# Spectral convolution: one column transform per group, and the first scale moved inside a group

## The chip, the cores and the metric

The kernel runs on one core of a Trainium2 chip. A core has five engines that work side by side, each from its own queue: TensorE (PE, with its weight loads PEld), VectorE (DVE), ScalarE (ACT), GpSimd (POOL) and SyncE (SP), which here only issues DMAs. The metric is the device time of one execution in microseconds (us). Times quoted from the profile are of one profiled execution, counted from the start of its span.

## The reference

Four layers in a row, each `x + layer(groupnorm(x))`, on x of 8 images, 32 channels, 256 × 256, float32:

1. a Fourier layer: two-dimensional real FFT, the lowest 32 × 32 frequencies of two corners mixed over the channels by complex weights, inverse FFT, plus a bias;
2. a 5 × 5 convolution with one kernel for all channels, padding 2;
3. a gated recurrence (GRU) along the image's width;
4. running maxima from four sides, mixed with x by a 1 × 1 convolution.

The group norm has 16 groups of two channels and takes mean and variance over a group's two channels and all pixels:

```python
def _gn(v, G=16, eps=1e-5):
    g = v.reshape(B_, G, C_ // G, H_, W_)
    m = jnp.mean(g, axis=(2, 3, 4), keepdims=True)
    s = jnp.var(g, axis=(2, 3, 4), keepdims=True)
    return ((g - m) / jnp.sqrt(s + eps)).reshape(v.shape)
x = x + _L0_conv_ref(_gn(x), ...)
x = x + _L1_conv_ref(_gn(x), L1_conv_kernel, 1, 2)
```

What the change touches is the end of layer 1 (the inverse transform) and the whole of layer 2 (the 5 × 5 convolution), which the kernel does in one stage.

## The kernel before

Stages follow each other: `forward_and_mix` (forward FFT and mixing, written to the scratch tensor smd), `inverse_and_conv` (the one concerned, about 305 to 1156 us of the span, its repeated part from 365 us), `recurrence` (to about 2530 us) and `maxima_and_mix`.

`inverse_and_conv` works on 16 *units*. A unit is half of one image's channels, 16 of them, in two channel halves `ch` of 8. A channel half lies in one of five large buffers (`x1s`, used in turn), laid out as nine *blocks* of 32 columns of the image on the partitions (four row phases `a` times 32), with 28 columns of progress from block to block, so that each block carries the margin that a 5 × 5 kernel needs.

For each unit:

- `load_spectrum` (once per image, so every second unit) brings the mixed spectrum from smd through SP's queue; `spectrum` then works on it with a few small VectorE instructions and one matmul, y0 (L367).
- `over_rows` (four calls of two channels) is the inverse transform along rows: four matmuls into tp (L407), copied to tt by ACT (L414).
- `over_columns` (one call per block p, called by `transform`) is the inverse transform along columns: eight matmuls into two PSUM banks "up" (L424), one per channel half, and then two VectorE additions (L433) that add the input x (loaded as xb through POOL's queue, L386) and write block p of the two x1 buffers. For p = 0 `transform` also issues eight small squares on ACT (L450), and for p = 2, 5 and 8 it starts the loads of a piece of x for the unit after (L386).
- `squares` sums x1² over blocks on ACT (L450), four activations (one per channel pair) per call. `scale` sums these over the partitions by matmuls into v (L457), adds eps on VectorE (ve, L461) and raises to the power −0.5 on POOL (r, L463). `r` is what the convolution's result is multiplied by; `spectrum` has already taken the mean out of the zero frequency.
- `conv(u, ch, g)` is one *group*: the 5 × 5 convolution of the two channels of pair g, as 18 tile matmuls of 64 × 64 on both halves of the array (L490, 36 instructions) into three banks vp, in an order of tiles written by hand and with a semaphore of its own. Five VectorE instructions (L527), called the *update* below, multiply by r, add to x1 in place and sum. A unit has eight groups: g = 0 to 3 for ch 0, 4 to 7 for ch 1.
- `squares2` (three ACT instructions, L534) sums the squares of the result of each group, `statistics` and `keep` make the next layer's mean and scale of them (L559 to L578), and `store` writes a channel half to x2d in HBM with 36 DMAs (nine blocks, four row phases a; L547), on SP's queue.

The work of three units overlaps: while unit u is convolved, the columns of unit u+1 are transformed and the rows of unit u+2. The whole stage stands in a `manual_schedule`: each engine executes its instructions in the order in which the program issues them. That order is the loop at the end of the function, over units u and groups g. `PLACES` says after which groups which column transforms of unit u+1 are placed: in the kernel before, one right behind the group's tiles, and in groups 1 to 3 a second one later in the same group. Unit u+1's first scale comes after group 7 of unit u, its second in group 1 of unit u+1 itself.

PSUM's eight banks are given by tags: four for vp, two for up, one for tp (tag "s"), one for all small sums (tag "st": v, y0 and the statistics' s). A tile of a tag waits until the reader of the buffer's last tile is done. A transform needs two banks of "up" at once. Likewise, writing a block of x1 waits for the stores that read the same block of the same buffer, five channel halves earlier.

## Time and profile before

| | us |
|---|---|
| median of 3 timed executions (lowest, highest) | 3231.57 (3227.11, 3237.39) |
| the profiled execution: span from first to last instruction | 3226.3 |
| forward transform and mixing, start of the stage | 0 to 365 |
| convolution stage, repeated part with its last stores | 365 to 1156 |
| recurrence | 1160 to 2530 |
| maxima and mixing | 2530 to 3226 |

The profiled execution's own time is given only as its span; the timed executions lie 0.8 to 11.1 us above it. Busy time in the window from 365 to 1160 us (795 us):

| engine | busy us | what fills it |
|---|---|---|
| PE | 727.8 | vp (L490) 453.3; up (L424) 185.7; tp (L407) 60.7 |
| DVE | 549.2 | update (L527) 350.8; sums of transforms (L433) 173.8 |
| ACT | 454.5 | squares2 (L534) 203.6; squares (L450) 166.4 |
| POOL | 113.9 | issue of loads, powers |

How to read the profile: a row of the order of time gives start, length, engine, line, operation, result <- operands, form, the number of merged instructions, and in square brackets how long the engine had stood idle and what released it. PE's busy time overlaps with itself a little, since matmuls are pipelined and their ends are modelled. A window's row gives, after its length, each engine's busy time, then the mean granted clock of TensorE (1.00 is full), the DMA engines' busy share and GB/s. "SPq" rows are DMA issues on SP's queue, from the first issue to the last.

### The profile page before, as it was taken

The numbers are of one execution on the slowest core, as the hardware profiler recorded it, in microseconds if no ns is written. First come the engines' busy times: TensorE is split into PE (matmuls) and PEld (weight loads), VectorE is DVE, ScalarE is ACT, GpSimd is POOL, SyncE is SP. The second block draws the span as 40 slices with busy tenths as digits, with TensorE's granted clock in tenths as the row PEclk, the third lists the DMA queues.
The fourth block names the chain that finished last, engine by engine and source line by source line (L and its number), as shares of the span: only waits on it lengthen the run. The fifth ranks groups of instructions, "written<-read, shape, count | busy, mean of one in ns | idle before, by whom it ended". The sixth has DMA issues, their size and how long they took to land.

```text
span 3226.3 us, 112014 instructions
## 1 busy us (share of the span) xinstructions
PE 2866.3 (89%) x47802; PEld 1666.4 (52%) x47802; DVE 2614.3 (81%) x5188; ACT 1862.5 (58%) x4362; POOL 860.8 (27%) x1241
## 2 busy tenths in 40 slices
PE   7975799999999969999999999999999577777776
PEld 4655344444444446666666666666666233333332
DVE  5742577777767759999999999999999799999998
ACT  3422365565565657888888888888887222222222
POOL 0110011111111145555555555555555200000000
PEclk9985899999999989999999999999999788888998
DMA  9978577888777545665555555666554588878885
GB/s 385 387 288 193 129 187 193 196 194 195 186 182 197 138 110 153 159 159 151 146 148 147 147 146 151 157 159 159 155 143 121 188 306 305 308 311 314 313 308 217
DMA packets 527058, 655.75 MB, mean 203 GB/s; under 512 B 388825, under 2 KB 389737, under 8 KB 500829
## 3 DMA queue, kind: packets, MB, share of 16 engines
q1 hardware_dynamic: 483628, 494.33, 53.9%
q0 software_dynamic: 17200, 85.05, 8.1%
q10 hardware_dynamic: 25728, 69.21, 5.4%
q8 instruction: 374, 6.13, 0.8%
q14 instruction: 128, 1.04, 0.1%
HBM read 371.63 MB, written 272.63 MB: 200 GB/s over the span
## 4 chain that ended last, share of the span: by engine, by line
PE 54%; DVE 25%; DMA 8%; SPq 6%; issue 5%; ACT 2%; POOL 0%; DVEq 0%; ACTq 0%; POOLq 0%
PE r L742 13%; PE z L742 12%; PE ni L742 6%; PE nh L742 6%; DMA x2d<-x 6%; SPq L547 5%; DVE rv L993 5%; PE vp L490 4%; DVE x L527 3%; PE yp L131 3%; DVE dq L1005 2%; DVE m L1009 2%; DVE m L1007 2%; DVE x L1002 2%; DVE m L1008 2%
## 5 line engine op out<-in xcount | busy, mean ns | idle before, releaser
L750 PE MATMUL z<-hs,weights 64*64 64x256 f32 x4080 | 539.4, 382 | 0.0
L750 PE MATMUL r<-hs,weights 64*64 64x256 f32 x4080 | 525.2, 375 | 0.0
L750 PE MATMUL ni<-hs,weights 64*64 64x256 f32 x4080 | 524.9, 375 | 0.0
L832 POOL TENSOR_TENSOR xw<-xw,hs 128x256 f32<-128x256 f32 x496 | 339.5, 684 | 635.6 <-DVE hs L831 635.6
L527 DVE SCALAR_TENSOR_TENSOR x<-vp,r,x 64x512 f32<-64x512 f32 (+2 forms) x640 | 350.8, 563 | 164.6 <-PE vp L490 137.8
L1039 ACT ACTIVATE ot<-o,bres 128x512 f32<-128x512 f32 x256 | 155.4, 690 | 541.5 <-PE o L1023 533.9
L490 PE MATMUL vp<-x,c_conv 64*64 64x384 f32 (+2 forms) x4608 | 457.5, 514 | 0.2
L826 POOL TENSOR_TENSOR a<-zm,xn 128x256 f32<-128x256 f32 x510 | 372.7, 731 | 6.4 <-issue 6.2
L1023 PE MATMUL o<-m,wsc 32*32 32x512 f32 x3072 | 237.1, 830 | 152.9 <-DVE m L1009 106.3
L824 ACT ACTIVATE n<-n,bih 128x256 f32<-128x256 f32 x510 | 260.8, 511 | 184.4 <-DVE n L823 184.4
L490 PEld LDWEIGHTS vp<-x,c_conv 64*64 64x64 f32 x4608 | 238.3, 138 | 234.5 <-issue 128.5
L742 PE MATMUL z<-xn,weights 64*64 64x256 f32 x2040 | 305.3, 376 | 24.2 <-ACT xn L722 24.2
L742 PE MATMUL r<-hs,weights 64*64 64x256 f32 x2040 | 319.0, 389 | 4.4 <-DVE hs L831 3.4
L742 PE MATMUL r<-xn,weights 64*64 64x256 f32 x2040 | 305.6, 376 | 1.0 <-ACT rs L817 1.0
L742 PE MATMUL nh<-xn,weights 64*64 64x256 f32 x2040 | 305.7, 376 | 0.0
L742 PE MATMUL z<-hs,weights 64*64 64x256 f32 x2040 | 305.2, 376 | 0.0
L742 PE MATMUL ni<-hs,weights 64*64 64x256 f32 x2040 | 305.2, 375 | 0.0
L722 ACT ACTIVATE xn<-xw,shift,turned 128x256 f32<-128x256 f32 x496 | 291.9, 589 | 0.0
L750 PEld LDWEIGHTS ni<-hs,weights 64*64 64x64 f32 x4080 | 284.4, 133 | 0.3
L818 DVE SCALAR_TENSOR_TENSOR n<-nh,bhh,rs 128x256 f32<-128x256 f32 x510 | 246.3, 483 | 45.3 <-ACT rs L817 30.7
L750 PEld LDWEIGHTS r<-hs,weights 64*64 64x64 f32 x4080 | 281.1, 131 | 0.2
L817 ACT ACTIVATE rs<-r,brz 128x256 f32<-128x256 f32 x510 | 242.7, 476 | 50.8 <-PE r L750 30.3
(165 smaller groups left out, 6267.2 us busy)
## 6 DMA issues: line engine op xcount, KB each, us to landing
xb<-in_xl_dram POOLq DMA_DIRECT2D x96, 768.0 KB, 6.4
xa<-in_xt_dram SPq DMA_DIRECT2D x64, 1024.0 KB
x<-x3d SPq DMA_DIRECT2D x32, 2048.0 KB
fw<-fwd SPq DMA_DIRECT2D x32, 2048.0 KB
out_dram<-ot ACTq DMA_DIRECT2D x64, 1024.0 KB
xw<-x2d SPq DMA_DIRECT2D x31, 2048.0 KB
fwd<-fm SPq DMA_DIRECT2D x248, 256.0 KB
x3d<-xw SPq DMA_DIRECT2D x248, 256.0 KB
```

Of the source, the lines that this page charges most:

```text
L490: ins = nc.tensor.matmul(vps[bank][to], lhsT=k.conv[r, P : P + 64] if kind == 2 else k.conv[r, o], rhs=pair_of(u, ch, g, lo, hi, (2, 0)[i] ...
L527: nc.vector.scalar_tensor_tensor(x, src[o], r1[rows, g : g + 1], x, ALU.mult, ALU.add, accum_out=s1[rows, 0, n, ch, g : g + 1])
L547: (nc.gpsimd if 2 * u + ch == 2 * n - 1 and p % 2 else nc.sync).dma_start(out=x2d[b, a, c0 : c0 + CH, TS * t + lo : TS * t + hi].rearrange ...
L722: nc.scalar.activation(norms[bi][:, b, w], raws[bi][:, b, w], AF.Identity, bias=shift[:, b : b + 1], scale=sc[:, 1, b : b + 1])
L742: ins = nc.tensor.matmul(out[r], lhsT=weights[r, kind, gate, :], rhs=src[r], start=start, stop=stop)
L750: ins = nc.tensor.matmul(out[pairs[1 - i]], lhsT=weights[r, kind, gate, :], rhs=prev[r, :, q0 : q0 + Q], start=False, stop=stop,)
L817: rs = nc.scalar.activation(r, p["r"], AF.Sigmoid, bias=brz[:, 0:1])
L818: nc.vector.scalar_tensor_tensor(m, p["nh"], bhh[:, 2:3], r, ALU.add, ALU.mult)
L824: nc.scalar.activation(m, m, AF.Tanh, bias=bih[:, 2:3])
L826: product = nc.gpsimd.tensor_tensor(a, zm, cur, ALU.mult)
L832: nc.gpsimd.tensor_tensor(raw, raw, new, ALU.add)
L1023: nc.tensor.matmul(pts[b2][i][32 * j : 32 * j + 32].rearrange("p (w q) -> p w q", q=Q), lhsT=wsc[q, b2, t, :], rhs=src[j][q, b2], start=first,
```

## The change

The order of work in the convolution stage is rearranged:

- `PLACES` becomes one block per group: after group 0 to 6 come blocks 1, 2, 3, 5, 6, 7, 8 of unit u+1. Block 4 is transformed *inside* group 3, between the group's tiles (`between`). Block 0 is begun a group early: of unit u+2, after group 7 of unit u.
- The banks: tp joins the small sums in one bank "st", and "up" gets three instead of two.
- Unit u's scale of channel half 0 is computed inside its own group 0, after 14 of the 18 tiles, and no longer after group 7 of the unit before. It now sums three pieces, so the squares of channel half 0 come in three: block 0, blocks 1 to 5 (in group 4) and blocks 6 to 8 (in group 7), where there were two (block 0, blocks 1 to 8 in group 5).
- `spectrum` moves from group 2 of an even unit to group 7 of the odd one before it (for the first image it stays in group 2 of unit 0), and `load_spectrum` from group 7 of the odd unit to its group 2, so ahead of the store of that unit's first half in SP's queue. `keep` moves by one group.
- A store issues its DMAs block by block, the four row phases of a block after each other; before, it went through all nine blocks for each row phase.

```diff
--- before.py
+++ after.py
@@ -314,7 +314,7 @@
     BANKS = ((0, 2), (2, 6), (6, 9))
     PIECES = ((0, 3), (3, 6), (6, 9))
 
-    PLACES = ((0,), (1, 2), (3, 4), (5, 6), (7,), (8,), (), ())
+    PLACES = (1, 2, 3, 5, 6, 7, 8)
     with ExitStack() as ctx:
         one = ctx.enter_context(tc.tile_pool(name="a2c", bufs=1))
         xp = ctx.enter_context(tc.tile_pool(name="a2x", bufs=1))
@@ -397,7 +397,7 @@
                 r=[None, None],
             )
 
-        def over_rows(u, c, tag="s", bufs=1):
+        def over_rows(u, c, tag="st", bufs=1):
 
 
             b, h = units[u]
@@ -413,7 +413,7 @@
                     )
             nc.scalar.copy(state[u]["tt"][:, :, c : c + 2, :], tp.rearrange("p c (a q) -> p a c q", a=A))
 
-        def over_columns(u, p, tag="up", bufs=2):
+        def over_columns(u, p, tag="up", bufs=3):
 
 
             tt = state[u]["tt"]
@@ -472,7 +472,7 @@
             if some[0]:
                 tc.declare_no_dep(ins.ins, group="conv", reason="later matmuls of the same bank end last")
 
-        def conv(u, ch, g):
+        def conv(u, ch, g, between=()):
 
 
 
@@ -511,6 +511,8 @@
             tiles(0, 1, start=True)
             tiles(2, 0, stop=True, wait=second)
             third = tiles(0, 2, signal=True)
+            for work in between:
+                work()
             tiles(1, 0, stop=True, wait=first)
             tiles(0, 0, stop=True, wait=third)
             s1 = state[u]["s1"]
@@ -541,9 +543,9 @@
         def store(u, ch):
             b, h = units[u]
             c0 = 2 * CH * h + CH * ch
-            for a in range(A):
-                for p, t in enumerate(BLOCKS):
-                    lo, hi = 0 if t == 0 else 2, 32 if t == NT - 1 else 30
+            for p, t in enumerate(BLOCKS):
+                lo, hi = 0 if t == 0 else 2, 32 if t == NT - 1 else 30
+                for a in range(A):
                     (nc.gpsimd if 2 * u + ch == 2 * n - 1 and p % 2 else nc.sync).dma_start(
                         out=x2d[b, a, c0 : c0 + CH, TS * t + lo : TS * t + hi].rearrange("c w q -> w c q"),
                         in_=x1_of(u, ch)[32 * a + lo : 32 * a + hi, p, :, 1 : 1 + Q],
@@ -579,7 +581,7 @@
                     by_pair(stb[:, kind, b, 2 * CH * h : 2 * CH * (h + 1)]), twice(st[:, kind], 2)
                 )
 
-        def transform(u, p, again):
+        def transform(u, p):
             if u:
                 over_columns(u, p)
             else:
@@ -587,10 +589,10 @@
             if p == 0:
                 for ch in range(2):
                     squares(u, ch, 0, 0, 1)
-            if again < n:
+            if u + 1 < n:
                 for i, (_, hi) in enumerate(PIECES):
                     if p == hi - 1:
-                        load(again, i)
+                        load(u + 1, i)
 
         n = len(units)
         with tc.manual_schedule(engines=None):
@@ -602,9 +604,9 @@
             for u in range(2):
                 begin(u)
             for c in range(0, CH, 2):
-                over_rows(0, c, *(("s", 1), ("up", 2))[c // 2 % 2])
+                over_rows(0, c, *(("st", 1), ("up", 3))[c // 2 % 2])
             for p in range(NT):
-                transform(0, p, 1)
+                transform(0, p)
                 if p % 2:
                     over_rows(1, p - 1)
                 if p == 4:
@@ -612,40 +614,49 @@
                         squares(0, ch, 1, 1, 5)
             for ch in range(2):
                 squares(0, ch, 2, 5, NT, ch == 1)
-                scale(0, ch, 3)
+            scale(0, 1, 3)
+            transform(1, 0)
             for u in range(n):
+                more, beyond = u + 1 < n, u + 2 < n
                 for g in range(2 * G):
-                    conv(u, g // G, g % G)
-                    places = PLACES[g] if u + 1 < n else ()
-                    for p in places[:1]:
-                        transform(u + 1, p, u + 2)
-
+                    between = []
+                    if g == 0:
+                        between.append(lambda: scale(u, 0, 3))
+                    if g == 3 and more:
+                        between.append(lambda: transform(u + 1, 4))
+                    conv(u, g // G, g % G, between)
+                    if g < len(PLACES) and more:
+                        transform(u + 1, PLACES[g])
+                    if g == 2 * G - 1 and beyond:
+                        transform(u + 2, 0)
                     if g == 1 and u > 0:
                         scale(u, 1)
-                    if g == 2 and u > 0:
-                        st = statistics(u - 1)
-                    if g == G - 1 and u + 2 < n:
-                        begin(u + 2)
-                    if G - 1 <= g < 2 * G - 1 and u + 2 < n:
-                        over_rows(u + 2, 2 * (g - G + 1))
-                    for p in places[1:]:
-                        transform(u + 1, p, u + 2)
-                    squares2(u, g // G, g % G)
                     if g == 2:
                         if u > 0:
-                            keep(u - 1, st)
-                        if u % 2 == 0 and u + 2 < n:
+                            st = statistics(u - 1)
+                        elif beyond:
                             spectrum(units[u + 2][0])
-                    if g == 5 and u + 1 < n:
-                        squares(u + 1, 0, 1, 1, NT)
-                    if g == 7 and u % 2 and u + 3 < n:
-                        load_spectrum(units[u + 3][0])
+                    if g == G - 1 and beyond:
+                        begin(u + 2)
+                    if G - 1 <= g < 2 * G - 1 and beyond:
+                        over_rows(u + 2, 2 * (g - G + 1))
+                    squares2(u, g // G, g % G)
+                    if g == 3 and u > 0:
+                        keep(u - 1, st)
+                    if g == 4 and more:
+                        squares(u + 1, 0, 1, 1, 6)
+                    if g == 7 and more:
+                        squares(u + 1, 0, 2, 6, NT)
+                    if u % 2 and u + 3 < n:
+                        if g == 2:
+                            load_spectrum(units[u + 3][0])
+                        elif g == 7:
+                            spectrum(units[u + 3][0])
                     if g % G == G - 1 and (u, g) != (n - 1, 2 * G - 1):
                         store(u, g // G)
                     if u == n - 1 and g == G:
                         nc.gpsimd.dma_start(out=flat(first[:, 0 : B - 1]), in_=first_columns(x2d, 0, B - 1))
-                if u + 1 < n:
-                    scale(u + 1, 0)
+                if more:
                     squares(u + 1, 1, 1, 1, NT)
             keep(n - 1, statistics(n - 1))
             store(n - 1, 1)
```

## The prediction

> **What bounds the kernel now.** I read the page's chain first, then busy time unit by unit, then one unit's order of time on each engine, then the store queue. The page's chain:

> ```profile
> PE r L742 13%; PE z L742 12%; PE ni L742 6%; PE nh L742 6%; DMA x2d<-x 6%; SPq L547 5%; DVE rv L993 5%; PE vp L490 4%; DVE x L527 3%; PE yp L131 3%; DVE dq L1005 2%; DVE m L1009 2%; DVE m L1007 2%; DVE x L1002 2%; DVE m L1008 2%
> ```

> The convolution stage (365 to 1156 us of the span) is there through the stores (x2d<-x, SPq L547), the tiles (vp) and their update (x L527). Three of its sixteen units, in the windows view (busy us and instructions of PE, PEld, DVE, ACT, POOL; clock; DMA):

> ```profile
> 659.70:708.80 49.10, 46.49 (x494) 21.70 (x488) 35.79 (x114) 29.39 (x85) 7.00 (x9) 0.97 0.86 198
> 708.80:755.50 46.70, 44.49 (x492) 20.80 (x486) 34.15 (x107) 29.36 (x85) 6.99 (x9) 1.00 0.74 196
> 755.50:805.80 50.30, 48.07 (x494) 22.29 (x488) 35.89 (x114) 29.39 (x85) 6.99 (x9) 0.93 0.84 190
> ```

> PE is the fullest engine, and the units differ by its clock. Order of time on PE, in the unit with clock 1.00:

> ```profile
> 710.12 3.38 PE L490 MATMUL vp<-x,c_conv 64*64 64x512 f32 x36
> 713.43 1.09 PE L424 MATMUL up<-tt,c_gw 64*32 64x512 f32 x16
> 714.45 0.61 PE L457 MATMUL v<-sq,c_valid 128*128 128x4 f32 x4
> 716.33 1.68 PE L424 MATMUL up<-tt,c_gw 64*32 64x512 f32 x16 [1.27 <-DVE x L433]
> 717.94 3.39 PE L490 MATMUL vp<-x,c_conv 64*64 64x512 f32 x36
> 722.28 1.73 PE L559 MATMUL s<-s,c_valid 128*128 128x8 f32 x14
> ```

> A group of tiles takes 3.32 us to what follows, a transform (up) 1.02, a scale's v about 0.53. The second transform of a group waits for DVE to empty the two "up" banks, so a group with two takes 7.82. Starts in that unit, group by group: 4.35, 7.82, 7.83, 7.82, 5.35, 5.35, 4.34, 3.85, in all 46.7. The other units add a clock dip or two:

> ```profile
> 617.00:620.42 3.42, 2.15 (x28) 0.83 (x20) 2.49 (x9) 3.17 (x18) 0.74 (x1) 1.00 0.60 126
> 620.42:623.83 3.41, 3.41 (x27) 2.01 (x24) 1.29 (x2) 3.25 (x11) 1.38 (x3) 0.50 0.66 119
> ```

> A window in which PE stood idle for a third is followed by one at half clock, and 36 matmuls then take 4.97 instead of 3.38 us. From the update of unit 0's last group (410.08) to unit 13's (1051.64) the mean unit is 49.35 us. The last view is the issuing queue of the stores:

> ```profile
> 567.87 92.67 SPq L547 DMA_DIRECT2D x2d<-x  x144
> 660.63 6.54 SPq L357 DMA_DIRECT2D spec<-smd  x4
> 667.27 90.68 SPq L547 DMA_DIRECT2D x2d<-x  x144
> ```

> SP issues stores without a break: from 469.23 to 967.10 ten units, 49.8 us each. It is as slow as the computation, and DVE was held by a store once (2.9 us).

> [...]

> **The change, part by part.**

> *One transform per group, the ninth inside group 3, three banks.* PE per unit has 8 × 3.32 + 9 × 1.02 + 4 × 1.01 (tp) + 0.53 (v of L457) + 1.66 (s, as in unit 15 where no transform follows it) = 41.97 us. With a third bank, and a full group between two transforms, no transform waits: the bank is emptied 6.2 us after its group began, the next transform comes 8.6 after. The transform inside group 3 finds the third bank free, the one behind it waits about 0.1. The old waits, 46.7 − 42.0 = 4.7 us a unit, go, and so do the dips (49.35 − 46.7 = 2.6). The loads that a transform starts on POOL's queue move with it: the third pair from group 5 to 6, past no pow, with six groups left until its use; nothing.

> *The scale inside group 0.* This is the price. The last squares of channel half 0 (blocks 6 to 8, four activations) are queued on ACT at the end of group 7, behind the squares of transform (u+2, 0) and behind squares2 of group 7. ACT in the unit boundary before, for the durations:

> ```profile
> 707.32 0.31 ACT L534 ACTIVATE junk<-x 128x128 f32<-128x128 f32 x1
> 709.28 1.07 ACT L450 ACTIVATE junk<-x 128x1024 f32<-128x1024 f32 x1
> 714.08 0.31 ACT L450 ACTIVATE junk<-x 128x128 f32<-128x128 f32 x1
> 717.58 0.31 ACT L534 ACTIVATE junk<-x 128x128 f32<-128x128 f32 x1
> ```

> squares2 takes 1.96 (707.32 to 709.28), the eight small squares 3.50 (714.08 to 717.58). Clock from the start of group 7's tiles: its update runs 2.73 to 5.48; the transform's first sum (0.68) ends at 6.16; ACT starts at 6.26, eight squares to 9.76, squares2 to 11.72, four squares of 384 columns (0.66 each, between 0.44 for 128 and 0.77 for 512) to 14.35. PE has reached the three v matmuls at 4.34 + 2.58 = 6.92, so it stands 7.6 us at the third. Queued behind it on PE are group 0's last tiles, transform 1 and group 1; on DVE the whole update. Then v 0.26, ve and pow (in the trace 1.38 from ve to the update, with POOL's 1.03): the update starts at 16.2, so last update to first update is 13.5 us where it was 4.15. Next behind it on ACT are the squares for the second scale: done at 19.2, PE comes to them at about 20.9, so they hold nothing unless ACT slips by 2 more. PE's unit: 41.97 + 0.26 + 0.3 for bank waits + 7.6 = 50.1 us.

> *The clock after that wait.* 7.6 us idle cover a whole window wherever the grid lies, so PE resumes at half clock for the rest of a window[...]. Loss: 0.95 to 2.65 us, depending on phase; I take 1.7. A unit: 51.8 us, 2.45 more than 49.35.

> *Squares in three pieces.* Four more activations on ACT, 1.3 us a unit; ACT is busy 29.4 of 49, so nothing beyond the boundary above.

> *One bank for tp, y0, v and s.* Each use finds the last one read: tp's copy runs about 0.7 after it and the next use is a group later. Nothing; if ACT's copy were late, tp would stand by as much.

> *Spectrum moved to group 7 of odd units, its load ahead of a store.* The load (5.2 us on SP) only changes places with 36 stores and lands some 20 us before its use. y0 (0.57) and DVE's 2 us fall into the wait. In even units spectrum cost 0.75 before (8.58 against 7.83 in unit 6), which the mean holds.

> *Stores block by block.* The same 36 issues of about 0.42 us and the same packets. Block 0, first read by the new early transform, is issued in the first four, about 10 us before that transform's sum; before, its last quarter was the 28th. Order costs nothing unless the four neighbours[...] land more slowly: from nothing to about 2 us a unit hidden in SP's slack (51.8 − 49.8), beyond that one for one.

> *Ends.* Unit 0 has no boundary wait behind it: first update about 1 later, its groups as above, last update at 401.0 instead of 410.1: −9.0. Units 1 to 13: 13 × 2.45 = +31.9. Unit 14 has no tp (−4.04) but the full wait: −0.7 + 1.7 = +1.0. Unit 15's boundary lacks the transform, so ACT is done at 10.1 and the update starts at 12.0: +4.4, less 1.6 that its scale no longer waits later: +2.8. Sum +26.7 on the span of 3226.3. The timed runs lie 0.8 to 11.1 above that span, the median 5.3; I leave that as it is and take 3231.6 + 26 = 3258.

> **Rivals.** (a) *The wait costs no more than the gain*: same place, but half the dip is covered and the mean unit is about 49.9 to 50.2; with −9 and +2 at the ends 3232 to 3240. For it: update and PE are within 1 us of each other after the wait. Against it: PE is the longer of the two. (b) *The store queue becomes the bound, and it is faster*: if ACT ran its squares before PE came to v (wait under 5 us), computation would take 43 to 47 us and SP's 49.8 would decide; the middle units gain nothing, unit 0 gives −9 and the queue's pauses in the last two units (2.4, 4.0 and 1.1 us) up to −7: 3216 to 3222. Against it: ACT's order, which puts 8.1 us of work behind a sum that ends at 6.2. (c) *Stores land more slowly in the new order*: SP over 52 a unit, DVE held at L433 more than once; 2 us a unit more gives 3280 to 3300. [...]against it 1136 stores that issue at 0.42 us.

> **How the numbers follow.** Forecast 0.62 (3242 to 3278), (a) 0.15, (b) 0.11, (c) 0.12. The range leaves out most of (b) and half of (c): 3225 to 3284. Within 0.3%, about what a measurement can tell from no change, lies (a) and a little of the forecast's low end: same 0.16, faster 0.11, slower 0.73.

> **What would show it.** ACT's eight small squares, squares2 and four squares of 384 stand in a row before v, and PE idles 7 to 8 us in the first group of each unit, "released by ACT junk L450"; clock 0.50 once or twice a unit, there only; the up matmuls wait for DVE nowhere else; units of 51 to 53 us; SP with pauses for data. The prediction is wrong if that idle time is under 5 us, or if SP still runs without pause.

## The result, and the profile after

| | before | after |
|---|---|---|
| median, us (lowest, highest) | 3229.34 (3225.89, 3237.39) | 3261.16 (3258.94, 3264.4) |
| span of the profiled execution, us | 3226.3 | 3257.2 |

The ratio of the times is 1.0094, with a 95% interval from 1.0076 to 1.0111: the changed kernel is slower by 0.9%, or 32 us. The forecast was 3258 (3242 to 3278).

In the chain of waits on the page of the kernel after, the stores have lost ground, and the tiles (vp) and ACT's squares have come in:

```profile
PE r L753 13%; PE z L753 12%; PE vp L490 9%; PE ni L753 6%; PE nh L753 6%; DVE rv L1004 5%; PE up L424 3%; SPq L549 3%; PE yp L131 3%; ACT junk L450 2%; DVE dq L1016 2%; DVE m L1020 2%; DVE m L1018 2%; DMA x2d<-x 2%; DVE x L1013 2%
```

Before, x2d<-x had 6%, SPq 5%, vp 4%. The convolution stage's end is now set by PE and by what PE waits for. That wait is seen in PE's order of time at a unit boundary; group 7's tiles begin at 710.47, those of the next unit's group 0 at 714.80:

```profile
710.47 3.38 PE L490 MATMUL vp<-x,c_conv 64*64 64x512 f32 x36
713.78 1.09 PE L424 MATMUL up<-tt,c_gw 64*32 64x512 f32 x16
714.80 2.60 PE L490 MATMUL vp<-x,c_conv 64*64 64x512 f32 x28
717.34 0.61 PE L457 MATMUL v<-sq,c_valid 128*128 128x4 f32 x4
724.79 0.59 PE L457 MATMUL v<-sq,c_valid 128*128 128x4 f32 x2 [6.85 <-ACT junk L450]
725.32 1.97 PE L490 MATMUL vp<-x,c_conv 64*64 64x512 f32 x8
```

Two of the three sums of v are done by 717.95; the third waits 6.85 us. The same stretch on ACT:

```profile
716.74 0.31 ACT L450 ACTIVATE junk<-x 128x128 f32<-128x128 f32 x1 [3.74 <-DVE x L433]
...
720.22 0.31 ACT L536 ACTIVATE junk<-x 128x128 f32<-128x128 f32 x1
...
722.17 0.53 ACT L450 ACTIVATE junk<-x 128x384 f32<-128x384 f32 x1
...
724.56 0.18 ACT L450 ACTIVATION_READ_ACCUMULATOR junk<-x 128x1 f32 x1
```

ACT stands idle until block 0 of unit u+2 has its first sum (716.74). Then come its eight small squares (3.48 us), squares2 (1.95), and the four squares of 384 columns (2.57) that v waits for. A row of the waits view says who waited, for whom, and then the us in total, how many times, and the longest. In the stage after the change the wait at v stands there once for each boundary:

```profile
PEld v L457 <- ACT junk L450: 95.1, 15, 6.9
PE v L457 <- ACT junk L450: 93.8, 15, 6.9
DVE x L433 <- PE up L424: 31.5, 14, 2.3
PEld up L424 <- DVE x L433: 11.3, 14, 0.8
```

The old waits of the up matmuls for DVE have gone. The same view of before has two rows for them, one of the weight loads and one of PE itself; after, only the weight loads wait (11.3 us in all), and no row of PE is left:

```profile
PEld up L424 <- DVE x L433: 73.8, 93, 2.7
PE up L424 <- DVE x L433: 38.5, 36, 1.8
```

Three units of after in the windows view (columns as in the prediction), and then two stretches at half clock, which begin in the wait:

```profile
673.70:726.80 53.10, 46.25 (x490) 20.95 (x488) 34.05 (x106) 30.53 (x93) 7.01 (x9) 0.92 0.66 175
726.80:779.00 52.20, 45.77 (x492) 20.77 (x490) 35.80 (x114) 30.58 (x93) 7.01 (x9) 0.93 0.80 189
779.00:830.70 51.70, 44.84 (x490) 20.49 (x488) 34.03 (x106) 30.51 (x93) 7.01 (x9) 0.93 0.69 181
```

```profile
722.33:729.16 6.83, 4.37 (x30) 1.09 (x30) 2.44 (x8) 6.61 (x15) 1.03 (x1) 0.50 0.60 125
...
824.73:834.97 10.24, 6.25 (x38) 2.19 (x42) 4.13 (x13) 9.86 (x25) 1.03 (x1) 0.50 0.56 121
```

How SP stands is told by its own waits, from 365 to 1110 us, first before, then after (DMA x2d<-x is a wait for an earlier store):

```profile
SPq L547 <- DMA x2d<-x: 77.1, 67, 3.1
SPq L547 <- DVE x L527: 71.5, 7, 62.1
```

```profile
SPq L549 <- DVE x L529: 105.4, 16, 55.3
SPq L549 <- DMA x2d<-x: 64.7, 52, 3.2
```

The longest wait for the update (62.1, 55.3) is the start of the stage. Without it, SP waited for the update 9.4 us in six waits before, and 50.1 us in fifteen after, 3.3 each. SP now has slack.

Summed from the starts of the updates:

| stretch | before | after | difference | predicted |
|---|---|---|---|---|
| to the last update of unit 0 | 410.1 | 399.0 | −11.1 | −9.0 |
| from there to that of unit 13 | 641.6 (49.35 a unit) | 680.4 (52.34) | +38.9 | +31.9 |
| unit 14 | 46.8 | 47.8 | +1.0 | +1.0 |
| unit 15 | 33.1 | 36.1 | +3.0 | +2.8 |
| the rest of the span | | | −0.9 | 0 |
| span | 3226.3 | 3257.2 | +30.9 | +26.7 |

### The profile page after: what moved, and what is told of

Same layout as the page of the kernel before. It is cut to its first block, busy times and chain, and to the rows that moved or that the text cites. A ratio compares the mean times of both kernels' runs of the same rounds, so it can differ in the third digit from the quotient of the medians.

```text
span 3257.2 us, 112292 instructions
## 1 busy us (share of the span) xinstructions
PE 2845.2 (87%) x47832; PEld 1652.7 (51%) x47832; DVE 2612.6 (80%) x5188; ACT 1875.6 (58%) x4482; POOL 862.2 (26%) x1241
## 4 chain that ended last, share of the span: by engine, by line
PE 61%; DVE 21%; DMA 5%; issue 4%; SPq 4%; ACT 3%; DVEq 0%; POOL 0%; ACTq 0%; POOLq 0%
PE r L753 13%; PE z L753 12%; PE vp L490 9%; PE ni L753 6%; PE nh L753 6%; DVE rv L1004 5%; PE up L424 3%; SPq L549 3%; PE yp L131 3%; ACT junk L450 2%; DVE dq L1016 2%; DVE m L1020 2%; DVE m L1018 2%; DMA x2d<-x 2%; DVE x L1013 2%
## 5 line engine op out<-in xcount | busy, mean ns | idle before, releaser
L490 PE MATMUL vp<-x,c_conv 64*64 64x384 f32 (+2 forms) x4608 | 463.6, 509 | 0.1
L490 PEld LDWEIGHTS vp<-x,c_conv 64*64 64x64 f32 x4608 | 222.6, 135 | 210.8 <-issue 118.9
L536 ACT ACTIVATE junk<-x 128x128 f32<-128x128 f32 (+1 forms) x384 | 202.9, 528 | 132.0 <-DVE x L529 122.9
```

Of the source, the lines that this page charges most:

```text
L490: ins = nc.tensor.matmul(vps[bank][to], lhsT=k.conv[r, P : P + 64] if kind == 2 else k.conv[r, o], rhs=pair_of(u, ch, g, lo, hi, (2, 0)[i] ...
L536: nc.scalar.activation(junk[:, : 2 * (hi - lo)], pair_of(u, ch, g, lo, hi), AF.Square, accum_out=state[u]["s1"][:, 1, n, ch, g : g + 1],)
```

## The experiments

All but three start from the kernel after; ratios are to the kernel before, measured again beside each run (medians 3228 to 3231 us). Here a unit counts from its first update to the first of the next.

**The squares ahead of the transform.** Does ACT's order make the wait, and what would stand behind it? The last squares of channel half 0 are issued ahead of group 7, so ahead of the transform of unit u+2 and of squares2 of group 7:

```diff
+                    if g == 7 and more:
+                        squares(u + 1, 0, 2, 6, NT)
                     conv(u, g // G, g % G, between)
...
-                    if g == 7 and more:
-                        squares(u + 1, 0, 2, 6, NT)
```

> The changed kernel with one edit: the four squares of blocks 6 to 8 of channel half 0 (ACT) are issued ahead of group 7's tiles and not at its end. Theory (ACT's order makes PE wait at the third v): the wait of 6.9 us per unit goes to under 1, half-clock windows at the unit boundary go with it, PE's unit could be about 43 us and the store queue becomes the next limit at 47 to 50 us a unit; total 3185 to 3222, below both kernels. Rival (stores in the new order, or the shared bank, cost the time): the total stays at 3250 to 3265, units at 51 to 53 us.

Measured: 3229.38 us, ratio 0.9993 (0.9983 to 1.0003). The wait went: where nothing else holds it, group 7 to the next update takes 6.4 to 7.3 us, not 13.6, and even units take 43.5 to 46. But the odd units from 3 to 11 take 55 to 59. In the waits view stores and the spectrum's load appear as holders:

```profile
DVE x L433 <- DMA x2d<-x: 47.7, 7, 12.2
PEld y L367 <- issue: 44.2, 7, 10.7
PE y L367 <- DMA spec<-smd: 38.1, 5, 9.9
```

and SP's order of time has one pair of units after the other:

```profile
647.16 94.38 SPq L549 DMA_DIRECT2D x2d<-x  x144
741.63 10.93 SPq L357 DMA_DIRECT2D spec<-smd  x4
752.65 91.33 SPq L549 DMA_DIRECT2D x2d<-x  x144
```

From 441.86 to 956.18 five pairs take 514.3 us, 51.4 a unit. SP waits for the update only 4.8 us in all, the start left out. So the wait at v is ACT's order, as forecast, and behind it the store queue is the bound. The expectation put the total too low (3185 to 3222): it had SP at 47 to 50 us a unit, near its pace of before, 49.8, but the load of the spectrum took 7.9 to 11.1 us on SP where it had taken 5.1 to 6.5.

**Half a dose.** The eight small squares of block 0 (3.5 us of ACT) are taken out of the row and issued behind the four that v waits for. `small` is a new function that holds the two lines taken out of `transform`:

```diff
-            if p == 0:
-                for ch in range(2):
-                    squares(u, ch, 0, 0, 1)
+            if p == 0 and u < 2:
+                small(u)
...
                     if g == 7 and more:
                         squares(u + 1, 0, 2, 6, NT)
+                    if g == 7 and beyond:
+                        small(u + 2)
```

> The changed kernel with one edit: the eight small squares of transform (u+2, 0) are issued on ACT behind the four squares of blocks 6 to 8 and not ahead of squares2, a dose of 3.5 us out of the row that stands before v. Theory (the wait is the length of ACT's row): PE's wait at v falls from 6.9 to about 3.4 us, last to first update from 13.6 to about 10.1, units from 52.3 to 47.5 to 49.5 if the store queue lets them, total 3205 to 3232. Rival (the wait has another cause, such as the shared bank of tp and the small sums): wait and total stay, 3255 to 3265.

Measured: 3226.14 us, ratio 0.9985 (0.9977 to 0.9992). Waits view:

```profile
PE v L457 <- ACT junk L450: 27.8, 13, 3.4
DVE x L433 <- DMA x2d<-x: 25.7, 4, 9.7
PE y L367 <- DMA spec<-smd: 16.4, 3, 9.2
```

The longest wait fell from 6.9 to 3.4 us, by the 3.5 taken out, and group 7 to the next update from 13.6 to 9.06 in units that no store holds. Units take 46 to 49 us, except five odd ones of 49.5 to 56 that stores or the spectrum hold. Halving the wait at v is enough to reach the store queue; the squares ahead of the transform, which take it away whole, gained nothing more.

**PE kept busy in the wait.** This separates the idle time from the clock. Seven matmuls on zeros, work that the kernel doesn't need, are put on PE ahead of the scale in group 0; `idle` is a new function that issues them, 128 × 128 by 512 columns, into the free third bank of up:

```diff
                     if g == 0:
+                        if u > 0:
+                            between.append(lambda: idle(u))
                         between.append(lambda: scale(u, 0, 3))
```

> The changed kernel with seven idle matmuls of 128 x 128 by 512 columns (on zeros, into the free third bank, read by nobody) between group 0's tiles and the scale's v, so that PE works through most of its wait. Theory (the clock term): the interval from last to first update stays at 13.5 to 13.7 us, the half-clock windows of the stage go, the interval from the first to the second update falls from 4.6 to 6.0 us to about 4.05, units from 52.3 to 50.0 to 50.8, total 3232 to 3242. Rival (the clock is not what stretches group 0 and 1): total 3255 to 3270.

Measured: 3238.69 us, ratio 1.0023 (1.0016 to 1.0031). The windows view over the stage, after and then with PE kept busy:

```profile
365.00:1185.00 820.00, 704.31 (x7533) 323.10 (x7524) 542.92 (x1721) 467.97 (x1408) 114.11 (x147) 0.92 0.70 174
```

```profile
365.00:1165.00 800.00, 768.87 (x7764) 356.26 (x7762) 542.69 (x1723) 468.00 (x1408) 114.45 (x148) 0.99 0.72 178
```

The units from 2 to 13 now take 50.5 us each (50.48 on average, counted as in the table of the result): 3.97, 4.45, 8.20, 4.41, 5.35, 5.35, 5.35, 13.41. The row on ACT is as long as ever, since the last interval lost only 0.2. What went is the half clock in groups 0 and 1: 52.34 − 50.48 = 1.86 us a unit, and 22.5 us of the time. It is 70% of what the change lost.

**The store's order undone.** The four row phases are the outer loop again:

```diff
-            for p, t in enumerate(BLOCKS):
-                lo, hi = 0 if t == 0 else 2, 32 if t == NT - 1 else 30
-                for a in range(A):
+            for a in range(A):
+                for p, t in enumerate(BLOCKS):
+                    lo, hi = 0 if t == 0 else 2, 32 if t == NT - 1 else 30
```

> The changed kernel with one edit undone: stores go through all nine blocks for each row phase again. Theory: the wait at v stays; block 0 is now complete only with the 28th of 36 stores, about 19 us after the batch began, so the early transform's second sum is held by a store for 0 to 5 us in some units: total 3260 to 3300. Rival (the new order of stores is what costs): total falls back to 3225 to 3240.

Measured: 3284.57 us, ratio 1.0167 (1.0147 to 1.0187); 23 us above the kernel after. Waits view:

```profile
DVE x L433 <- DMA x2d<-x: 22.1, 7, 5.0
```

This row is absent after the change. Block 0 of unit u+2 is now written right after group 7, and in the old order it comes free only with the 28th of 36 stores. Six units, five of them odd, take 14.9 to 17.6 us from group 7 to the next update, and ACT's row starts that much later.

**The store's order alone.** The same edit the other way round, on the kernel before:

> The kernel before with one edit: stores go block by block, the four row phases of a block after each other. Theory: order of the issues costs nothing by itself; total within 8 us of the kernel before, SP's runs of 144 stores stay at 91 to 98 us, and the one hold of 2.9 us of DVE by a store goes. Rival[...]: SP's runs grow by 4 us or more, and the total by 20 to 60 us.

Measured: 3236.62 us, ratio 1.0017 (1.0009 to 1.0026). By itself the order brings nothing; it costs some 6 us. The batches of 144 stores were no slower (91.2 to 95.7 us, before 90.7 to 97.5), and the one hold of DVE by a store was gone, but the spectrum's load was late for y0:

```profile
PEld y L367 <- issue: 17.8, 5, 4.8
...
PE y L367 <- DMA spec<-smd: 12.4, 4, 3.4
```

and SP's pairs took about 102.3 us where they had taken 99.6. Why the load takes longer in this order I did not find out.

**SP relieved of the spectrum.** With the squares first, the spectrum's loads go to POOL's queue:

```diff
-                    nc.sync.dma_start(
+                    (nc.gpsimd if b > 1 else nc.sync).dma_start(
                         out=t[64 * ri : 64 * ri + 64, :, ro], in_=smd[b, ri ^ ro].rearrange("s x o y -> (s x) o y")
                     )
```

> The squares-first kernel (blocks 6 to 8 squared ahead of group 7's tiles) with one more edit: from the third image on, the spectrum's loads are issued on POOL's queue and not on SP's. Theory (with the wait at v gone the store queue is the limit, and it is long because a spectrum load of 8 to 11 us stands in it every second unit): the matmul y0 no longer waits (38 us in five waits), SP's pairs of units fall from 102.5 to 91 to 95 us, units to 45 to 47.5, total 3165 to 3205, below both kernels. Rival (the DMA engines and not the order in the queue are the limit): the stores' runs grow by what the spectrum leaves, total 3220 to 3232.

Measured: 3209.18 us, ratio 0.9932 (0.9917 to 0.9947). The waits for the spectrum are gone; the stores still hold DVE:

```profile
DVE x L433 <- DMA x2d<-x: 19.0, 5, 5.5
```

From unit 2 on, even units take 44.6 to 46 us, odd ones 47 to 54. The time lies just above the range of the theory (3165 to 3205), since SP's stores alone still hold the computation.

**SP relieved of a sixth of its stores too.** Of the first half's stores, one block in three goes to POOL's queue:

```diff
-                    (nc.gpsimd if 2 * u + ch == 2 * n - 1 and p % 2 else nc.sync).dma_start(
+                    (nc.gpsimd if (p % 2 if 2 * u + ch == 2 * n - 1 else ch == 0 and p % 3 == 2) else nc.sync).dma_start(
```

> As the run with the spectrum on POOL's queue, and one store in three of channel half 0 (12 of a unit's 72) goes to POOL's queue too. Theory: SP has 12 issues fewer a unit (5 to 7 us), so it is no longer the limit and PE is, units at 43.5 to 45, total 3150 to 3185. Rival (POOL's queue, where a store's issue takes 0.62 us, delays the loads of x and the powers): total 3200 or more.

Measured: 3171.36 us, ratio 0.9819 (0.9805 to 0.9834), faster than both kernels. No store holds DVE in the stage. What is left at v:

```profile
PE v L457 <- ACT junk L450: 20.9, 14, 2.1
```

These are the squares of the second scale, in group 1. From unit 2 on, units take 44.6 (even) and 45.5 to 48.1 us (odd), where the expectation had 43.5 to 45.

**What the relief alone does.** Three runs put the same relief on other orders, to see whether it would have been a gain by itself: the spectrum on POOL in the kernel before; that with the store's new order and the sixth of the stores on POOL; and the full relief in the kernel after.

> The kernel before with the spectrum's loads on POOL's queue from the third image on, a control. Theory: there PE's waits and the clock set the unit and SP only keeps pace with it, so nothing is gained but the one hold by a store: within 10 us of the kernel before. Rival (SP set the pace before the change already): 15 us or more faster.

> The kernel before with stores block by block, the spectrum's loads and one store in three of channel half 0 on POOL's queue: SP relieved, the order of transforms and scales as before. Theory (two limits, PE's waits for the two up banks and SP's queue, lie close together before): units of 46.7 to 50 us as PE and the clock set them, no hold by stores, total 3205 to 3228. Rival (relieving SP's queue alone gives the gain of the run with part of the stores on POOL): total under 3190.

> The changed kernel with SP relieved in the same way, the squares of blocks 6 to 8 where the change put them. Theory (SP is not the limit of the changed kernel, ACT's row before v is): units stay at 51.7 to 53.1 us, total within 8 us of the changed kernel, 3253 to 3269. Rival (SP's queue costs the changed kernel time): total 3240 or less.

Measured, in this order: 3234.3 us, ratio 1.001 (0.9999 to 1.0021); 3215.13, 0.9955 (0.9938 to 0.9971); 3259.75, 1.0092 (1.0073 to 1.0112). All three lie in the ranges of their theories. In the first, SP issues stores only, but they hold DVE five times, where the expectation had even the one hold of before (2.9 us) gone:

```profile
DVE x L433 <- DMA x2d<-x: 16.4, 5, 4.2
```

In the third, every interval between updates is that of the kernel after to within 0.1 us, so SP isn't what sets its time. The four together:

| | SP as it was | SP relieved |
|---|---|---|
| order of before (relieved: stores by block) | 3229 | 3215 |
| order of after | 3261 | 3260 |
| order of after, squares first | 3229 | 3171 |

In the changed order the wait at v has to go and SP has to be relieved: the first alone is worth 32 us, the second alone 1, both 90. With SP relieved, the changed order with its squares first is 44 us faster than the order of before (3171 against 3215), so the rearrangement does gain once the wait that came with it is gone. Its parts (one transform per group, the third bank of up, the shared bank st) were not run one by one.

## Why the prediction was right

**One transform per group, the ninth inside group 3, three banks.** Right in kind: PE no longer stands still for the up banks. At the one place named, behind the transform inside group 3, the weight loads wait 0.81 us for DVE, but PE meanwhile has the last tiles of the group and goes on without a gap. What the forecast left out is that a group cut in two takes PE longer. From 738 to 757 us of after, group 3 and the whole group behind it:

```profile
739.98 2.61 PE L490 MATMUL vp<-x,c_conv 64*64 64x512 f32 x28
742.52 1.09 PE L424 MATMUL up<-tt,c_gw 64*32 64x512 f32 x16
743.54 1.09 PE L490 MATMUL vp<-x,c_conv 64*64 64x512 f32 x8
744.56 1.09 PE L424 MATMUL up<-tt,c_gw 64*32 64x512 f32 x16
...
746.59 3.39 PE L490 MATMUL vp<-x,c_conv 64*64 64x512 f32 x36
749.91 1.09 PE L424 MATMUL up<-tt,c_gw 64*32 64x512 f32 x16
```

The parts take 2.54 and 1.02 us to what follows, 3.56 together, and the whole group 3.32. Group 0, cut for the scale, has the same parts in the run with PE kept busy. Two cuts are 0.48 us a unit, and that is the size of what is to be explained: the seven intervals within a unit at full clock take 37.08 us in that run, the forecast had 36.6 (50.1 − 13.5). No run took a cut away by itself.

**The scale inside group 0.** Right, and by its steps. From the start of group 7's tiles: ACT starts at 6.27 (forecast 6.26), the eight squares take 3.48 (3.50), squares2 1.95 (1.96), the four of 384 columns 2.57 (4 × 0.66), and the row is done at 14.27 (14.35). Last update to first update takes 13.61 us (13.5). The wait itself is 6.9 and not 7.6 us, because the forecast began it at 6.92, before PE's first two sums for v, which last 0.6, and ended it at 14.52 (6.92 + 7.6) where it ended at 14.32; nothing follows from that, since the row's end decides. The half dose shows that this row is the cause: the wait fell by just what was taken out of it. "The squares for the second scale" hold nothing here, as forecast; once the row is gone they are the next wait (2.1 us).

**The clock after that wait.** Right in size and in where it falls: 1.7 forecast, 1.86 by the run with PE kept busy (1.26, 1.70 and 2.63 us in units of 51.74, 52.18 and 53.11 us; the range had 0.95 to 2.65). The range and the 1.7 were the author's estimate. How much work in one window at half clock still lets a second one follow, the trace of before did not settle: it has one such pair, with 1.69 of 3.41 us worked in the first (from 913.96). In the kernel after PE worked 2.87 of 3.42 us in one, and the next was at half clock too; after one with 3.39 the clock was full again:

```profile
671.13:674.55 3.42, 2.87 (x18) 1.03 (x26) 0.99 (x4) 3.33 (x7) 1.03 (x1) 0.50 0.57 126
674.55:677.96 3.41, 3.41 (x28) 1.18 (x16) 3.14 (x10) 3.28 (x9) 0.00 (x0) 0.50 0.38 81
...
776.95:780.36 3.41, 3.39 (x26) 1.03 (x26) 1.51 (x5) 3.35 (x6) 1.03 (x1) 0.50 0.63 124
780.36:783.77 3.41, 3.41 (x50) 1.79 (x36) 2.82 (x11) 3.17 (x10) 0.00 (x0) 1.00 0.52 118
```

Half of the half-clock time in which PE works is 2.2, 3.1 and 1.7 us at the three kinds of boundary (722.33, 667.72 and 773.53), 2.3 in the mean, and about 0.5 less than that is lost, 1.70, 2.63 and 1.26; why less, no run shows. So that 1.7 came so near is partly luck. Nor do a window idle for a third and a dip always go together in the kernel before. Between 400 and 1110 us PE was busy for 2.15 us or less in 14 windows at full clock; 13 are followed by a dip, the one from 470.23 (2.14 us) by full clock. Of the 19 dips there, six follow a window in which PE was busy for about 3.3 us, such as

```profile
429.28:432.69 3.41, 3.26 (x38) 1.95 (x30) 3.09 (x12) 1.87 (x6) 0.10 (x1) 1.00 1.01 338
432.69:436.10 3.41, 3.41 (x27) 1.84 (x24) 1.45 (x4) 0.00 (x0) 1.56 (x1) 0.50 0.61 129
```

How much work in a window keeps the clock up stays open.

Put together, a unit of before is 46.70 us at full clock and 2.65 of dips and of the spectrum in even units, 49.35. After, the intervals within a unit fall from 42.55 to 37.08 us (−5.5) and the one at the boundary rises from 4.15 to 13.41 (+9.3), which gives 50.5; the half clock adds 1.86, and that is 52.34, where the forecast had 50.1 + 1.7 = 51.8. The 0.54 over thirteen units are the 7 us by which the middle of the stage was short. Unit 0, which gained 2.1 more than said, hides a part of it, and that is luck: its first update came 1.5 us earlier than before (363.69, 365.15) and not 1 later, while from its first to its last update it gained 9.65, where the forecast had 10. In the runs built on the kernel after the first update lies anywhere from 363.7 to 367.7.

**Stores block by block.** Forecast as nothing, and as a cost if the new order landed more slowly (rival c). The sum is right only because the change has it: next to the early block 0 it saves 23 us, and by itself it costs some 6. The forecast named the mechanism (block 0 in the first four issues, "its last quarter was the 28th") without pricing what happens in the old order. Rival (c) is refuted in its cause: where SP was the bound (the squares ahead of the transform), batches of 144 stores in the new order took 91.3 to 94.6 us, before 90.7 to 97.5.

**Spectrum moved.** "Only changes places" held for this kernel, since its SP has slack. The price entered did not: the load takes 7.0 to 10.6 us on SP in the kernel after, where 5.2 was forecast. It costs nothing here, but counts where SP is the bound, as with the squares ahead of the transform.

**Rivals (a) and (b).** (a) needed units of 49.9 to 50.2; even at full clock a unit took 50.5. (b) was said to decide from a wait under 5 us. The half dose has 3.4 us and the store queue does hold units there: right on where it decides. The time it gave, 3216 to 3222, was 4 to 13 us low, because SP's pace rose from 49.8 to 51.4 a unit.

**The ends.** Units 14 and 15 were right to 0.2 us. In unit 15 two misses cancel: its boundary took 4.1 us more (4.4 forecast), its groups 1.1 less (1.6).

## What to carry to other kernels

Where a reduction is moved to just before its use, write out the queue of the engine that makes it: what is ahead of it there, and when the first of that can start, gave the end of the row here to 0.1 us, while ACT's busy share (31 of 52 us) didn't show it. Price an idle stretch of TensorE twice, for itself and for the half clock behind it: here 6.9 us of wait brought 1.86 us more. And look at how close the second bound lies: with stores as slow as the computation, mending the first wait gave 32 us, mending both 90.

## What the runs showed that I had not expected

Counted from last update to last update, the units of the changed kernel come in a cycle of three, 53.1, 52.2 and 51.7 us, from unit 3 to unit 13 without exception. Together they are 157.0 us, which is 46 windows of 3.413 us (10.24 over three). The half clock lasts 10.24, 6.83 and 6.83 us in them, at the same phase of the grid each time. With PE kept busy the cycle is gone and all units are equal (50.5 us). So the wait at each boundary did not spread evenly over the phases of the clock's windows; it seems locked to them. The link between the lock and its cause is argued from these numbers; no run shifted the phase by itself. The run with the store's order undone speaks for it: stores hold its units 2, 4, 6 and 8 (54.5 to 57 us), and units 3, 5, 7 and 9 to 11 still take 52.16, 53.16, 52.24, 53.25, 52.30 and 51.75 us.

The same load of the spectrum takes 5.1 to 11.3 us of SP's time, depending on what stores stand around it. It was the difference between the forecast pace of the store queue and the real one, and what makes it longer is open.
